# A graph network's layer ends: the third last superchunk's logits moved into the sums of its predecessor, and two merges moved behind a scaling

## The chip, the core and the metric

The kernel runs on one core of a Trainium2 chip. The core has five engines that work through lists of their own: TensorE (PE in the profile) for matrix products, VectorE (DVE) for elementwise work and scans, ScalarE (ACT) for activations and copies, GpSimd (POOL), which here only issues gathers, and SyncE (SP), which issues the other transfers. They wait for each other by semaphores. The metric is the device time of the whole program in microseconds, as the median over runs. One more execution is recorded by the profiler; its rows are what the prediction works with.

## The reference

The input is a graph of 6250 nodes with 256 features, and 200000 edges sorted by their target node, each with 32 features. Two attention layers run over it, the first with 4 heads, the second with 1. Cut to what matters:

```python
h = relu(layernorm(x))
for l in (0, 1):                        # heads 4 and 1
    te = relu(edge_attr @ We + be) * exp(h @ Wo + bo)[src][:, None]
    s2, d2, ea2 = add_self_loops(src, dst, te, n)     # loop: mean of te over a node's edges
    hx = (h @ Wg).reshape(n, H, F)
    al = leaky_relu((hx*a_s).sum(-1)[src] + (hx*a_d).sum(-1)[dst] + ((ea2@Wge).reshape(-1,H,F)*a_e).sum(-1), 0.2)
    al = exp(al - segment_max(al, dst)[dst])
    al = al / segment_sum(al, dst)[dst]
    out = segment_sum(hx[src] * al[:, :, None], dst) + b
    h = relu(out + h) if l == 0 else out + h + h_start
return x + h
```

So each edge needs a row of its source node, an attention logit, a softmax over all edges with the same target, and a weighted sum into that target.

## The kernel before

The sorted edges are cut into chunks of 128, and 24 chunks make a superchunk. There are 66 superchunks per layer, numbered s = 0 to 65; the last two are shorter, 17 chunks (64) and 10 chunks (65). One superchunk's edges reach at most 112 consecutive nodes, so that its weighted sums fit in one window of 128 rows.

For a superchunk the program does the following, and each step is a method of the class.

- `gather` issues one indirect transfer per chunk on POOL: 128 rows of the node table T of this layer, into the buffer G (line 1084). There are three G buffers, taken in turn.
- `nodes` loads the table rows and the inputs of the window's own nodes (`tw`, `xw`) by SP, into one of four places, taken in turn.
- `spread`, `parts`, `rphase1`, `rphase2`, `blocks` and `adst` build the edge part of the logits in the PSUM tile `zad`: comparisons and casts on DVE (lines 1210, 1211, 1325 to 1328), products on TensorE (1186, 1195, 1333, 1347), a relu on ACT (1187).
- `edge_rows` turns `zad` into rows per edge (1361) and sums parts (1365).
- `logits` forms the logits and scans them forwards and backwards within a partition (1377 to 1394). `ends` transposes the scans' ends on TensorE into the tile `lf` (1401). `links` scans these across partitions on DVE (1411, 1413) and has TensorE transpose the result back (1418). `maxima` takes the maximum per segment, ACT the exponential of the difference (1428 to 1452).
- `onehots` makes the matrix S that maps an edge to its row of the window (1312). `scale` multiplies G by the softmax weights (1483, in pieces if asked). `carried` adds what the predecessor had for a node that both share into the first row of G (1465 to 1473); it needs the predecessor's evicted sums.
- `sums` adds S times G over all chunks in PSUM (1495, two matmul records per chunk), `evict` copies the result to SBUF on ACT (1501).
- `finish` is the merge with the self loop: some twenty short operations on DVE and a few on ACT (lines 1512 to 1609). In layer 0 `rows1`, `rows2` and `rows3` then make the node's row for layer 1 (two transpositions, two products, an addition at line 575, an exponential) and store it by SP into T, into T1, which is a second copy of the table, and into two tables of window rows. In layer 1 `rows3` stores the output.

The order on every engine is the order in which these methods are called; nothing is rearranged by a scheduler. The method `edges` runs through the superchunks of layer 0 and then of layer 1. In step k it takes superchunk k from its logits to its sums, and beside that prepares the edge part of k+1 and merges k-1. The rows of k-1 are finished in step k+1 (the variable `late`).

The last three superchunks of a layer are taken together by `ending(a, b, c, pv, late, after)`: a is 63, b is 64, c is 65, pv is 62, late is 61, and after is the first superchunk of layer 1, or nothing at the end. Before the change the step of 62 ends with the merge of 61 and then the merge of 62, and `ending` begins with the logits of 63. At the first layer's end, 24 gathers for layer 1 are issued early, from T1, into the G buffer of 63 (`after["own"] = ... a["G"]`); they wait for the sums of 63 and for the stores of 61 and 62 into T1. The rows of the last three superchunks are not in T1 then. They are put in afterwards by products with a selection matrix, from rows of T that the last stores have written. The second superchunk of layer 1 is gathered from T and waits for the last of these stores.

`warm` issues a product whose result nobody reads. `index_on` makes the index tables of later superchunks in layer 0, some 14 short DVE operations at a time.

Of the kernel before, what the change touches and what calls it, by code (L numbers as in the profile page):

```python
# [81 lines left out]
class Kernel:  # L82
# [704 lines left out]
    def edges(self, ctx):  # L787
        nc = self.nc
        steps = self.steps
        if self.NS % 2:  # L790
            self.load_lb(1)
        pv = late = None
        self.ahead, self.rest = 1, None
        for k, st in enumerate(steps):
            nx = steps[k + 1] if k + 1 < len(steps) else None
            if st["s"] + 2 >= self.NS:
                continue
            for q in steps[k + 1:k + 3]:
                if q["L"] is st["L"] and "tw" not in q:
                    self.nodes(q)  # L800
            self.load_lb(k + 2)
            left = 99
            if self.ahead < len(self.groups):
                left = self.groups[self.ahead][0] - 2 - (self.ahead + 2 >= len(self.groups)) - k
            self.fresh = self.rest is None and left <= 3
            if self.fresh:
                gi = self.index_load(self.ahead, self.xp)
                self.rest = self.index_group(self.ahead, self.xp, gi)
            if st["L"].l and (st["s"] == 2 or st["s"] + 3 == self.NS) and not hasattr(self, "flag_i"):
                self.flag()  # L810
                if self.early:
                    self.window()
            if st["s"] + 3 == self.NS:
                self.ending(st, *steps[k + 1:k + 3], pv, late, steps[k + 3] if k + 3 < len(steps) else None)
                pv = late = None
                continue
            if k == 2:
                nx["own"] = steps[0]["G"]
            if k:
                if "G" not in nx:  # L820
                    self.gather(nx, st.get("behind"))
                drain(self.logits(st))
                self.ends(st)
                self.index_on(k, left, False)
            self.spread(nx)
            self.parts(nx)
            y = self.rphase1(nx)
            next(y)
            if k:
                self.links(st)  # L830
            if late:
                self.rows2(late)
            self.load_fl(k + 1)
            self.blocks(nx)
            if k:
                drain(self.maxima(st))
            drain(y)
            self.load_ea(k + 2)
            self.rphase2(nx)
            self.adst(nx)  # L840
            if "S" not in st:
                self.onehots(st)
            if k:
                drain(self.scale(st))
                self.carried(st)
                self.sums(st)
            if late:
                self.rows3(late)
                late = None
            self.onehots(nx)  # L850
            rows = self.edge_rows(nx)
            for gap in self.finish(pv) if pv else ():
                if gap:
                    next(rows, None)
            drain(rows)
            self.evict(st)
            if pv:
                self.rows1(pv)
                late = pv
            self.index_on(k, left, True)  # L860
            if k == 4 and self.early:
                self.lacking()
            if k >= 6:
                next(self.late, None)
                next(self.late, None)
            if st["s"] + 4 == self.NS:
                drain(self.finish(st))
            pv = st

    def index_on(self, k, left, late):  # L870
# [15 lines left out]
    def ending(self, a, b, c, pv, late, after):  # L886
# [10 lines left out]
        for q in () if after or self.early else (b, c):  # L897
            q["idx"] = idx = self.np_.tile([P, 1], I32, name="oidx")
            nc.vector.tensor_add(idx, self.base_f[:, q["s"]:q["s"] + 1], self.iota_m)
            nc.vector.memset(idx[0:1, :], 1 << 20)  # L900
        drain(self.logits(a))
        self.ends(a)
        self.spread(b)
        self.parts(b)
        y = self.rphase1(b)
        next(y)
        self.links(a)
        self.rows2(late)
        self.load_fl(k + 1)
        self.blocks(b)  # L910
        drain(self.maxima(a))
        self.rows3(late)
        drain(y)
        self.load_ea(k + 2)
        if after:
            self.warm(1, self.ps_1, "u", [P, 512])
        self.rphase2(b)
        self.adst(b)
        self.rows1(pv)
        if after:  # L920
            self.warm(1, self.ps_1, "u", [P, 512])
        n = a["C"]
        p, r = 5 * n // 12, n - 7
        drain(self.scale(a, cuts=(1, p, n)))
        drain(self.scale(a, cuts=(0, 1)))
        self.carried(a)
        self.rows2(pv)
        self.sums(a, (1, p))
        self.rows3(pv)
        drain(self.edge_rows(b))  # L930
        y = self.rphase1(c)
        next(y)
        self.sums(a, (p, p + 4))
        drain(y)
        self.load_ea(k + 3)
        self.sums(a, (p + 4, r))
        self.onehots(b)
        drain(self.logits(b))
        self.ends(b)
# [2 lines left out]
        self.rphase2(c)  # L942
        self.links(b)
        self.blocks(c)
        self.sums(a, (r, n), (0, 1))
        self.adst(c)
        if early:
# [920 lines left out]
```

## Time and profile before

| | us |
|---|---|
| median of the three runs | 4654.29 |
| lowest and highest of them | 4650.57, 4657.3 |
| the profiled execution | 4691.18 |
| span of its trace, first to last instruction | 4689.3 |

| engine | busy us | share of the span | instructions |
|---|---|---|---|
| PE | 2936.1 | 63% | 10096 |
| DVE | 2834.2 | 60% | 6211 |
| ACT | 534.1 | 11% | 1189 |
| POOL | 3000.1 | 64% | 3216 |

Every row in the prediction is from this one profiled execution. Rows of a timeline begin with the start in microseconds from the span's beginning and the duration; then come engine, line, operation, result and operands, shape and count; in brackets stands the time in which the engine was idle before it, and what ended that. "remote" and "another core or an unknown queue" mean that the profile doesn't show what ended it. Rows of the table by stretch begin with the stretch; then come its length, the busy time of PE, PEld, DVE, ACT and POOL with the number of instructions in brackets, the granted clock of TensorE as a share, the share of the transfer engines, and GB/s. In the page's groups the two figures behind the bar are the busy time in all and the mean of one in nanoseconds.

### The profile page before, as it was taken

What the parts mean: (1) busy time and instruction counts of PE and PEld (TensorE: products, weight loads), DVE (VectorE), ACT (ScalarE), POOL (GpSimd) and SP (SyncE); (2) the same over time, 40 slices, a digit from 0 to 9 for tenths busy, and PEclk for the clock granted to TensorE, in tenths of its full rate; (3) what the DMA queues carried; (4) which work ended last, traced back from release to release, by engine and by line L of the source; (5) the groups of instructions that cost most, each with busy time, mean ns of one, the idle gap of its engine ahead of it and who ended that gap; (6) DMA issues with size and microseconds to landing.
All of it is one profiled execution on the core that took longest, in us unless ns stands there. A gap on an engine that the chain in (4) does not pass through costs nothing.

```text
span 4689.3 us, 35036 instructions
## 1 busy us (share of the span) xinstructions
PE 2936.1 (63%) x10096; PEld 1851.6 (39%) x10096; DVE 2834.2 (60%) x6211; ACT 534.1 (11%) x1189; POOL 3000.1 (64%) x3216
## 2 busy tenths in 40 slices
PE   7766665666666666666666656656566565565656
PEld 5434343343343343343443333434334343343334
DVE  6666676676666666666665545545455554554546
ACT  4211111111111111111110000000000000000000
POOL 5466666666666666666646666666666666666664
PEclk8877777777777777777787767767767776767767
DMA  7344444444444444444444444444444444444442
GB/s 221 87 131 134 124 137 136 125 133 136 133 130 133 135 129 132 138 129 132 133 117 115 123 119 118 127 113 122 123 122 119 118 126 116 119 124 113 123 124 74
DMA packets 248234, 591.76 MB, mean 126 GB/s; under 512 B 65850, under 2 KB 105126, under 8 KB 247784
## 3 DMA queue, kind: packets, MB, share of 16 engines
q0 software_dynamic: 150048, 422.51, 34.2%
q1 hardware_dynamic: 97009, 164.82, 11.0%
q10 hardware_dynamic: 976, 2.12, 0.2%
q8 instruction: 81, 1.33, 0.1%
q14 instruction: 120, 0.98, 0.1%
HBM read 544.23 MB, written 45.36 MB: 126 GB/s over the span
## 4 chain that ended last, share of the span: by engine, by line
DVE 31%; PE 24%; issue 19%; another core or an unknown queue 14%; POOL 10%; ACT 1%; DMA 1%; SPq 0%; DVEq 0%; ACTq 0%; POOLq 0%
PE u L1495 16%; DVE G L1483 12%; POOL G L1084 10%; DVE S L1312 4%; PE y L1186 3%; DVE lb L1210 1%; DVE m L1433 1%; DVE rt L1361 1%; PE ps L570 1%; PE fin L570 1%; PE zad L1195 1%; DMA G<-T,src 1%; DVE al L1379 1%; DVE a3r L1326 1%
## 5 line engine op out<-in xcount | busy, mean ns | idle before, releaser
L1084 POOL DMA_INDIRECT G<-T,src x3066 | 2924.0, 954 | 1582.1 <-issue 886.6
L1495 PE MATMUL u<-G,S 128*128 128x270 f32 (+1 forms) x6212 | 1721.0, 435 | 763.5 <-issue 556.0
L1495 PEld LDWEIGHTS u<-G,S 128*128 128x128 f32 x6212 | 1319.2, 215 | 1100.2 <-issue 597.3
L1483 DVE TENSOR_TENSOR G<-G,kps 128x6144 f32<-128x6144 f32 (+6 forms) x149 | 854.1, 5739 | 0.0
L1186 PE MATMUL y<-ea,webd 64*128 64x256 f32 (+2 forms) x1056 | 454.5, 811 | 366.0 <-issue 353.2
L1411 DVE TENSOR_TENSOR_SCAN cl<-fl,cl,lf 4x129 f32<-4x129 f32 (+1 forms) x130 | 61.1, 470 | 855.4 <-remote 756.0
L1312 DVE TENSOR_TENSOR S<-kps,loc 128x3072 f32<-128x3072 f32 (+1 forms) x135 | 438.1, 3245 | 4.6
L1195 PE MATMUL zad<-R,wea 128*64 128x384 f32 (+1 forms) x1056 | 293.1, 694 | 155.4 <-ACT R L1187 98.2
L1186 PEld LDWEIGHTS y<-ea,webd 64*128 64x128 f32 x1056 | 161.6, 287 | 510.4 <-issue 493.3
L1501 ACT ACTIVATE U<-u 128x270 f32<-128x270 f32 (+1 forms) x130 | 51.0, 393 | 1959.1 <-remote 1409.1
L1187 ACT ACTIVATE R<-y,webd 128x1024 f32<-128x1024 f32 (+3 forms) x264 | 235.4, 892 | 329.9 <-PE y L1186 173.4
L1195 PEld LDWEIGHTS zad<-R,wea 128*64 128x64 f32 x1056 | 84.5, 180 | 410.4 <-issue 205.2
L1379 DVE TENSOR_TENSOR al<-G 128x96 f32<-128x96 f32 (+1 forms) x132 | 34.2, 259 | 236.6 <-remote 176.3
L570 PE MATMUL fin<-wg,h1T 128*128 128x260 f32 x264 | 126.3, 628 | 1.5 <-ACT h1T L1589 1.5
L1361 DVE STREAM_TRANSPOSE rt<-zad 128x768 f32<-128x768 f32 (+1 forms) x130 | 125.7, 967 | 2.4 <-PE zad L1347 2.4
L1333 PE MATMUL zad<-a,Q 128*128 128x12 bf16 (+1 forms) x132 | 24.4, 185 | 143.2 <-issue 103.5
L1401 PE MATMUL lf<-ident,fb 128*36 128x128 f32 (+1 forms) x132 | 46.0, 349 | 107.4 <-issue 62.7
L1210 DVE TENSOR_TENSOR lb<-lb,kps 128x1536 bf16<-128x1536 bf16 (+1 forms) x68 | 112.9, 1661 | 0.0
L1587 PE MATMUL fin<-ident,fb 128*128 128x128 f32 x132 | 45.0, 395 | 98.8 <-issue 97.0
L1587 PEld LDWEIGHTS fin<-ident,fb 128*128 128x128 f32 x132 | 24.7, 195 | 164.7 <-issue 160.1
L1526 ACT ACTIVATE mw<-mw,mg 128x2 f32<-128x2 f32 x66 | 19.7, 298 | 601.5 <-DVE mw L1522 529.7
L1347 PE MATMUL zad<-lb,aq 128*128 128x384 bf16 (+2 forms) x264 | 85.0, 414 | 0.0
(267 smaller groups left out, 2275.6 us busy)
## 6 DMA issues: line engine op xcount, KB each, us to landing
ea<-in_ea_dram SPq DMA_DIRECT2D x64, 768.0 KB
G<-T,src POOLq DMA_INDIRECT x3066
lb<-locrow SPq DMA_DIRECT2D x64, 384.0 KB
nd<-t1rows SPq DMA_DIRECT2D x66, 225.8 KB
tw<-nd SPq DMA_DIRECT2D x66, 225.8 KB
tw<-T SPq DMA_DIRECT2D x66, 117.2 KB
T<-t1rows SPq DMA_DIRECT2D x66, 113.8 KB
tw<-in_x_dram SPq DMA_DIRECT2D x66, 112.0 KB
```

The source lines that it names most:

```text
L570: self.product = self.nc.tensor.matmul(ps[:, :L.MW], hT[:, k, :], self.wg[L.l][:, k, :], start=(k == 0), stop=(k == 1))
L1084: g = nc.gpsimd.indirect_dma_start(out=G[:, c, 0:L.TW], out_offset=None, in_=st.get("from", self.T[L.l])[0:self.N, :], in_offset=bass.Indi ...
L1186: nc.tensor.matmul(y[:, i, :n], self.webd[l][r, :], ea[r, w], start=True, stop=True)
L1187: nc.scalar.activation(R[:, :, w], y[:, :, :n], AF.Relu, bias=self.be[l])
L1195: nc.tensor.matmul(st["zad"][i * PH:(i + 1) * PH, o], self.wea[l][0], R[:, i, w], start=True, stop=False)
L1210: V.tensor_tensor(lb[:, :, :n], lb[:, :, :n], self.k_part.unsqueeze(2).to_broadcast([P, i, n]), op=OP.is_equal)
L1312: nc.vector.tensor_tensor(st["S"][:, c0:c1, :], self.k_iota.unsqueeze(1).to_broadcast(w), self.loc[:, o + c0:o + c1].unsqueeze(2).to_broad ...
L1347: self.nc.tensor.matmul(st["zad"][:, o], st["aq"].rearrange("p k j -> p (k j)"), st["lb"][:, w], start=False, stop=True)
L1361: V.transpose(rv[:, :32 * c].rearrange("p (b n) -> p b n", b=2), z.rearrange("p (b n) -> p b n", b=2)[:, :, :16 * c])
L1379: V.tensor_add(zv, gr, G[:, :c, L.p:L.p + H])
L1483: nc.vector.tensor_tensor(v, v, pw[:, c0:c1, :].unsqueeze(3) .to_broadcast([P, c1 - c0, H, L.F]), op=OP.mult)
L1495: p = nc.tensor.matmul(st["u"][:, :L.W], S[:, i, :], G[:, i, 0:L.W], start=(j == 0), stop=(j == c - 1))
```

## The change

In the step of superchunk 62, the sums are issued in three parts, 16, 4 and 4 chunks. Between the parts go the edge rows, logits, ends and links of 63, and behind them its maxima. The merges of 61 and of 62 are no longer in this step. In `ending`, what stood at the head for superchunk 63 falls away, its scaling starts at once, and the two merges and the making of rows for 61 and 62 follow behind it, among the parts of 63's sums. The load of 65's node rows moves from the head of step 63 to behind the merge of 61, whose place in the ring it takes. The load of 64's and 65's flags moves into the step of 62. Two warm-up products of the first layer's end are dropped. It applies at the ends of both layers.

```diff
             for q in steps[k + 1:k + 3]:
-                if q["L"] is st["L"] and "tw" not in q:
+                if q["L"] is st["L"] and "tw" not in q and q["s"] + 1 < self.NS:
                     self.nodes(q)
...
-                self.sums(st)
+                self.sums(st, (0, 2 * C // 3 if st["s"] + 4 == self.NS else st["C"]))
...
             self.onehots(nx)
+            if st["s"] + 4 == self.NS:
+                drain(self.edge_rows(nx))
+                drain(self.logits(nx))
+                self.ends(nx)
+                self.sums(st, (2 * C // 3, 5 * C // 6))
+                self.links(nx)
+                self.sums(st, (5 * C // 6, C))
+                self.load_fl(k + 2)
+                drain(self.maxima(nx))
+                self.evict(st)
+                self.rest_left = left
+                late, pv = pv, st
+                continue
...
-            if st["s"] + 4 == self.NS:
-                drain(self.finish(st))
             pv = st
...
-        drain(self.logits(a))
-        self.ends(a)
+        n = a["C"]
+        p, r = 5 * n // 12, n - 7
         self.spread(b)
         self.parts(b)
         y = self.rphase1(b)
         next(y)
-        self.links(a)
-        self.rows2(late)
-        self.load_fl(k + 1)
         self.blocks(b)
-        drain(self.maxima(a))
-        self.rows3(late)
+        scaling = self.scale(a, cuts=(1, p, n))
+        next(scaling)
         drain(y)
         self.load_ea(k + 2)
-        if after:
-            self.warm(1, self.ps_1, "u", [P, 512])
+        self.sums(a, (1, p))
+        drain(scaling)
+        drain(self.scale(a, cuts=(0, 1)))
         self.rphase2(b)
         self.adst(b)
-        self.rows1(pv)
-        if after:
-            self.warm(1, self.ps_1, "u", [P, 512])
-        n = a["C"]
-        p, r = 5 * n // 12, n - 7
-        drain(self.scale(a, cuts=(1, p, n)))
-        drain(self.scale(a, cuts=(0, 1)))
+        rows = self.edge_rows(b)
+        for gap in self.finish(late):
+            if gap:
+                next(rows, None)
+        drain(rows)
         self.carried(a)
-        self.rows2(pv)
-        self.sums(a, (1, p))
-        self.rows3(pv)
-        drain(self.edge_rows(b))
+        self.nodes(c)
+        self.rows1(late)
+        self.sums(a, (p, p + 4))
+        self.rows2(late)
+        drain(self.finish(pv))
+        self.index_on(k, self.rest_left, True)
+        self.rows3(late)
         y = self.rphase1(c)
         next(y)
-        self.sums(a, (p, p + 4))
+        self.sums(a, (p + 4, r))
+        self.rows1(pv)
         drain(y)
         self.load_ea(k + 3)
-        self.sums(a, (p + 4, r))
+        self.rows2(pv)
         self.onehots(b)
         drain(self.logits(b))
         self.ends(b)
...
         self.links(b)
         self.blocks(c)
+        self.rows3(pv)
         self.sums(a, (r, n), (0, 1))
         self.adst(c)
```

## The prediction

> **What bounds the kernel now.** I read the page first, then the POOL and DVE timelines around the two layer ends, then the chain of waits and the busy time by stretch.
>
> ```profile
> span 4689.3 us, 35036 instructions
> L1084 POOL DMA_INDIRECT G<-T,src x3066 | 2924.0, 954 | 1582.1 <-issue 886.6
> L1312 DVE TENSOR_TENSOR S<-kps,loc 128x3072 f32<-128x3072 f32 (+1 forms) x135 | 438.1, 3245 | 4.6
> L1361 DVE STREAM_TRANSPOSE rt<-zad 128x768 f32<-128x768 f32 (+1 forms) x130 | 125.7, 967 | 2.4 <-PE zad L1347 2.4
> L1401 PE MATMUL lf<-ident,fb 128*36 128x128 f32 (+1 forms) x132 | 46.0, 349 | 107.4 <-issue 62.7
> ```
>
> A superchunk is 24 gathers of 0.95 us with 0.30 us between them (POOL rows below), 30 us, plus a wait for the sums that free the buffer: POOL paces the middle of both layers. The change leaves the 62 middle steps of each layer as they are. It can act only at the two layer ends (superchunk 63 is the third last, 64 the second last, 65 the last), and a shift at the first end moves all of layer 1 by the same amount.
>
> First end: the row before and after the gathers for layer 1, and the chain.
>
> ```profile
> 2382.72 0.94 POOL L1084 DMA_INDIRECT G<-T1e,src  x1 [20.35 <-PE zad L1347]
> ...
> 2411.66 1.10 POOL L1084 DMA_INDIRECT G<-T1e,src  x1 [0.30 <-issue]
> 2430.46 0.94 POOL L1084 DMA_INDIRECT G<-T,src  x1 [17.70 <-DMA T<-t1rows]
> ```
>
> ```profile
> 2400.19 10.10 another core or an unknown queue
> 2410.31 0.70 ACT R L1187
> ```
>
> POOL is idle 20.35 us until TensorE has finished the sums of 63; then come 24 gathers from T1, and then a wait for 65's rows in T. So what counts here is when the last sixteen matmuls of 63's sums end. What precedes them is DVE's list, from the one-hots of 63 to the links of 64, and in the second end the same list:
>
> ```profile
> 2336.64:2378.33 41.69, 32.38 (x135) 22.13 (x133) 35.16 (x104) 6.84 (x19) 15.79 (x17) 0.84 0.42 114
> 4617.93:4656.26 38.33, 26.43 (x119) 18.95 (x119) 26.61 (x65) 3.66 (x8) 18.31 (x20) 0.82 0.31 83
> ```
>
> The third busy figure is DVE's: 35.16 of 41.69 us, and 26.61 of 38.33. The new order permutes this list; it takes no work out of it. It can win only the idle part, and only where it does not put idle time elsewhere.
>
> **First end, part by part.** DVE's rows:
>
> ```profile
> 2346.23 0.45 DVE L1365 TENSOR_REDUCE ade<-rt 128x96 f32<-128x288 f32 x1 [0.99 <-DVE fa L1578]
> 2347.64 0.42 DVE L1582 SCALAR_TENSOR_TENSOR t1rows<-fa,t1rows 128x256 f32<-128x256 f32 x1 [0.96 <-DVE ade L1365]
> ...
> 2350.20 0.15 DVE L1512 TENSOR_SCALAR cnt<-U 128x1 f32<-128x1 f32 x1 [0.89 <-ACT U L1501]
> ...
> 2354.95 0.26 DVE L1377 TENSOR_TENSOR G<-rt,G 128x96 f32<-128x96 f32 x1
> ...
> 2356.77 0.69 DVE L1210 TENSOR_TENSOR lb<-lb,kps 128x544 bf16<-128x544 bf16 x1
> ...
> 2357.58 0.17 DVE L1325 CAST a<-tw 128x8 bf16<-128x8 f32 x1
> ...
> 2358.29 0.47 DVE L1411 TENSOR_TENSOR_SCAN cl<-fl,cl,lf 4x129 f32<-4x129 f32 x1
> ...
> 2377.39 0.47 DVE L1411 TENSOR_TENSOR_SCAN cl<-fl,cl,lf 4x129 f32<-4x129 f32 x1 [1.40 <-PE lf L1401]
> ```
>
> and TensorE's and ACT's:
>
> ```profile
> 2336.25 11.07 PE L1495 MATMUL u<-G,S 128*128 128x270 f32 x40 [3.00 <-DVE crow L1471]
> 2347.65 2.09 PE L1495 MATMUL u<-G,S 128*128 128x270 f32 x8 [0.33 <-issue]
> ...
> 2378.53 3.91 PE L1495 MATMUL u<-G,S 128*128 128x270 f32 x16
> ```
>
> ```profile
> 2349.77 0.40 ACT L1501 ACTIVATE U<-u 128x270 f32<-128x270 f32 x1 [1.71 <-PE u L1495]
> ```
>
> Waits that go: 0.99, 0.96, 0.89 and 1.40, together 4.24 us. Waits that come: with the one-hots (3.25), edge_rows of 63 (0.97 + 0.45) and its logits (2354.95 to 2356.77, 1.82) in a row, DVE is at 2343.1. The ends stand behind sixteen chunks of 62's sums, 32 matmuls at 11.07/40: 2345.1, plus 0.35 for the transposition, 2345.45. DVE waits 2.3 us. Its links take 0.94 (2377.39 to the window's end 2378.33), to 2346.4; the transposition back stands behind eight more matmuls, 2348.0: another 1.6 us. In the ending, blocks(b) comes straight behind parts(b) and waits for a product on TensorE with nothing between; no row has this pair alone, it is between 0 and the 0.7 that the casts take, I take 0.4. The casts for 65 (2357.58 to 2358.29, 0.7 us) become a second set, because 65's rows are no longer loaded when 64's casts run. The table row of 62 leaves the list (0.3). Sum: -4.24 + 2.3 + 1.6 + 0.4 + 0.7 - 0.3 = +0.5 us. The scaling starts some 9 us earlier, and both merges, the index steps and the table row of 61 are then done behind it: same work, same end.
>
> TensorE's two warm-up products go, the first part of 63's sums runs about 13 us earlier; what is left for the end is the same sixteen matmuls, 3.91 us behind the links of 64. ACT's pieces move with their merges and cost nothing while DVE leads. The two transpositions inside 62's sums delay the end of these by 0.7 us and so the ten gathers of 65; POOL's 20.35 us of idle time covers that.
>
> SP: 65's node rows (two loads) move from the start of step 63 behind the first merge, some 12 us ahead of the casts that read them; a landing is 3.4 us by the next rows, so they are covered, and would cost at most those 3.4. The flags' load moves forward behind 63's links; behind it wait only loads for layer 1. The four stores of 61 and of 62 come 9 us later. One of them is new on the path: 62's rows in T1, which the gathers at 2382.72 read, are now written behind the links of 64.
>
> ```profile
> 2369.80 0.41 DVE L575 TENSOR_TENSOR t1rows<-fin,bias 128x260 f32<-128x260 f32 x1
> ...
> 2427.06 0.43 DVE L575 TENSOR_TENSOR t1rows<-fin,bias 128x260 f32<-128x260 f32 x1 [0.46 <-PE fin L570]
> ```
>
> ```profile
> 2371.03 1.15 SPq L1630 DMA_DIRECT2D T1e<-t1rows  x1
> ```
>
> From a table row's start (2427.06) to the gather that its store releases (2430.46) it is 3.4 us; T1's store is the second one, 0.4 to 1.2 more. With 0.2 for blocks ahead, T1 is ready 4.0 to 4.8 us after the links; the sums are done 0.35 + 3.91 + 0.28 = 4.5 after. That is -0.5 to +0.3; I add 0.2. First end: **+0.7 us**, and everything behind it shifts along.
>
> **Second end.**
>
> ```profile
> 4621.21 0.21 DVE L1517 SCALAR_TENSOR_TENSOR mg<-U,cnt,tw 128x1 f32<-128x1 f32 x1
> ...
> 4633.01 0.22 DVE L1517 SCALAR_TENSOR_TENSOR mg<-U,cnt,tw 128x1 f32<-128x1 f32 x1 [7.99 <-ACT U L1501]
> ...
> 4636.29 0.20 DVE L1377 TENSOR_TENSOR G<-rt,G 128x24 f32<-128x24 f32 x1 [0.24 <-issue]
> ...
> 4641.57 6.67 DVE L1483 TENSOR_TENSOR G<-G,kps 128x2304 f32<-128x2304 f32 x3
> ...
> 4655.31 0.47 DVE L1411 TENSOR_TENSOR_SCAN cl<-fl,cl,lf 1x129 f32<-1x129 f32 x1 [1.29 <-PE lf L1401]
> ```
>
> ```profile
> 4617.88 10.83 PE L1495 MATMUL u<-G,S 128*128 128x261 f32 x48 [1.77 <-DVE G L1473]
> ```
>
> ```profile
> 4632.59 0.39 ACT L1501 ACTIVATE U<-u 128x261 f32<-128x261 f32 x1 [10.20 <-remote]
> ```
>
> Here there is something to win: 7.99 + 1.29 = 9.28 us of waits. But the 7.99 is odd: by the records 62's sums end at 4628.71, and ACT takes them only at 4632.59, 3.9 us later. In the middle of layer 1 the same is seen on the very wait that the change moves in here, the links' wait for the ends:
>
> ```profile
> 4596.94 0.27 PE L1401 MATMUL lf<-ident,fb 128*33 128x128 f32 x1
> ...
> 4608.05 0.39 ACT L1501 ACTIVATE U<-u 128x261 f32<-128x261 f32 x1 [20.19 <-remote]
> 4608.08 0.47 DVE L1411 TENSOR_TENSOR_SCAN cl<-fl,cl,lf 1x129 f32<-1x129 f32 x1 [16.45 <-remote]
> ```
>
> TensorE's record of the transposition ends at 4597.2, DVE gets it at 4608.08, together with ACT: a signal of TensorE is late while gathers run. After the change, logits of 63 end about 4623.4 (4617.93 + 3.25 + an estimated 2.2, the layer-0 pieces at a quarter of the width). The ends are recorded at 4617.88 + 10.83 x 32/48 + 0.35 = 4625.45.
> - Prompt signals: waits of 2.0 for the ends, 1.2 for the transposition back (eight matmuls of 0.23 and 0.35 later), 0.4 for blocks, 0.5 for edge_rows of 64 behind the first sums, and 0.7 of casts: -9.28 + 4.8 = -4.5 us.
> - All held until 4632.59: 9.2 + 0.4 + 0.5 + 0.5 + 0.7 - 9.28 = +2.0 us.
> - Each 3.9 late as the row shows, at the latest at 4632.59: 5.9 + 2.3 + 0.2 + 0.5 + 0.7 - 9.28 = **+0.3 us**. I take this one, since it is this stretch's own row.
>
> **Sum.** +0.7 + 0.3 = +1.0. The profiled execution (4691.18 us, 1.9 outside its span) would come to 4692.2; the median shown is 36.9 lower and the change is the same there: 4654.29 + 1.0 = **4655.3 us**.
>
> **Rivals.**
> - *Prompt signals in layer 1* (4.5 instead of 0.3): 0.7 - 4.5, 4650.5 us. For it: at 2349.77 ACT took 62's sums in layer 0 without delay. Against it: 4632.59 and 4608.08.
> - *A slow TensorE, on the other side.* Between the early sums and the last sixteen matmuls TensorE now mostly waits for DVE, and the warm-ups are gone. The profile shows what a gap does:
>
> ```profile
> 2350.00:2356.00 6.00, 0.00 (x0) 0.00 (x0) 5.11 (x23) 1.71 (x6) 4.77 (x5) 0.80 0.60 148
> 2356.00:2362.00 6.00, 3.97 (x13) 2.50 (x15) 5.39 (x21) 0.84 (x2) 4.47 (x6) 0.50 0.41 113
> ...
> 4583.30:4590.00 6.70, 6.65 (x17) 5.28 (x18) 6.12 (x13) 0.30 (x1) 5.09 (x6) 0.55 0.39 107
> ```
>
>   After six empty microseconds the granted clock is 0.50; at 0.55, 17 matmuls of the sums take 6.65 us, 0.39 each against 3.91/16 = 0.244. Sixteen cost 2.35 us more. In layer 0 that lies on the path to T1's gathers, in layer 1 ahead of the last superchunk's zad product, for which DVE waits: 4.7 us in all, 4660.0. It decides if the gap ahead of the sixteen is near the empty stretch of the row; I count about 3 us with only small products in it. [...]
> - *ACT is freed in the first end.* The 10.10 us in the chain are ACT waiting to read one more TensorE result while T1's gathers run; 65's sums follow. If the gathers start later against 64's work, that signal may be out before: up to 10.1 us, 4645.2.
>
> **How the numbers follow.** Forecast 0.40, prompt 0.30, slow TensorE 0.18, ACT freed 0.09, the rest unforeseen. This kernel's measurement can tell about 0.2% from no change, 4645.0 to 4663.6. Below lie half of ACT freed (0.045), a third of prompt, where other gains join it (0.10), and a twelfth of the forecast case (0.035): 0.18. Above lie a third of slow TensorE, where all signals are held as well (0.06), an eighth of the forecast case (0.05) and the unforeseen (0.03): 0.14. Within: 0.68. The range takes in ACT freed and the slow case with 3 us of spread: 4645 to 4663.
>
> **What would show it.** In the after trace: DVE's wait at line 1411's counterpart in step 62 (2.3 us in layer 0; 2.0, 5.9 or 9.2 in layer 1 tells prompt from held); the first gather from T1 within 1 us of where it was against the one-hots of 63, released by the sums or by T1's store; the granted clock in the last sixteen matmuls (1.00 or 0.5); ACT's 10.1 us still there. I am wrong if DVE's list is not the bound, or if the middle steps change their period.

## The result, and the profile after

| | median, us | lowest to highest | runs |
|---|---|---|---|
| before | 4654.29 | 4650.57 to 4661.45 | 11 |
| after | 4666.38 | 4658.14 to 4673.75 | 11 |

The change makes the kernel 0.26% slower: ratio 1.0026, 95% interval 1.0018 to 1.0034, or 12.1 us. The forecast was 4655.3 us, within 0.2% of no change, with a range of 4645 to 4663; the measured median lies 3.4 us above that range.

The two profiled executions cannot be compared as wholes. That of before took 4691.18 us, 37 us more than its median, and spread the excess over many middle steps, most of them in layer 0; that of after took 4673.75 us (span 4671.9). So I measure each layer end by itself, from the eviction of superchunk 61's sums to that of 63's. The lines of the changed kernel stand 12 further down behind `ending`. ACT's timeline at the two ends, before:

```profile
2323.25 0.40 ACT L1501 ACTIVATE U<-u 128x270 f32<-128x270 f32 x1 [10.84 <-PE u L1495]
...
2382.48 0.40 ACT L1501 ACTIVATE U<-u 128x270 f32<-128x270 f32 x1 [2.11 <-PE u L1495]
...
4660.28 0.39 ACT L1501 ACTIVATE U<-u 128x261 f32<-128x261 f32 x1 [2.67 <-PE u L1495]
```

and after:

```profile
2301.51 0.40 ACT L1513 ACTIVATE U<-u 128x270 f32<-128x270 f32 x1 [12.24 <-remote]
2329.48 0.40 ACT L1513 ACTIVATE U<-u 128x270 f32<-128x270 f32 x1
2366.26 0.40 ACT L1513 ACTIVATE U<-u 128x270 f32<-128x270 f32 x1 [4.32 <-PE u L1507]
...
4582.95 0.39 ACT L1513 ACTIVATE U<-u 128x261 f32<-128x261 f32 x1 [20.14 <-remote]
4612.39 0.39 ACT L1513 ACTIVATE U<-u 128x261 f32<-128x261 f32 x1 [2.60 <-PE zad L1345]
4643.07 0.39 ACT L1513 ACTIVATE U<-u 128x261 f32<-128x261 f32 x1 [4.76 <-PE u L1507]
```

The first end grows from 59.2 to 64.8 us (+5.5), the second from 52.2 (4608.05, shown in the prediction, to 4660.28) to 60.1 (+7.9). Together 13.4 us; the medians say 12.1. Most middle steps keep a period of 34 to 35 us, by the evictions (median 34.5 us before, 34.4 after).

Where each end grows is seen in DVE's list, in the same stretch as in the prediction: from the one-hots of 63 to the links of 64. The last two rows are the last sixteen matmuls of 63's sums at each end.

```profile
2314.89:2359.05 44.16, 34.45 (x129) 24.16 (x130) 35.02 (x106) 6.62 (x18) 15.54 (x17) 0.78 0.36 93
4592.84:4636.34 43.50, 29.43 (x117) 21.02 (x119) 27.02 (x68) 3.55 (x8) 18.09 (x20) 0.78 0.27 73
2359.90:2366.20 6.30, 6.30 (x19) 4.78 (x18) 4.26 (x10) 0.44 (x2) 0.00 (x0) 0.61 0.44 154
4637.10:4643.10 6.00, 6.00 (x19) 4.61 (x18) 3.33 (x8) 0.22 (x2) 0.00 (x0) 0.64 0.01 3
```

DVE has as much work as before (35.0 and 27.0 us busy; 35.16 and 26.61 before), but the stretches are 2.5 us (41.69) and 5.2 us (38.33) longer. What follows the links is 3.1 and 2.7 us longer: (64.75 - 13.38 - 44.16) - (59.23 - 13.39 - 41.69), and (60.12 - 9.89 - 43.50) - (52.23 - 9.88 - 38.33). That splits both losses into longer waits of DVE and slower last matmuls.

DVE's waits, from its timeline at the first end,

```profile
2326.16 0.47 DVE L1423 TENSOR_TENSOR_SCAN cl<-fl,cl,lf 4x129 f32<-4x129 f32 x1 [4.71 <-PE u L1507]
...
2343.94 0.81 DVE L1371 STREAM_TRANSPOSE rt<-zad 128x288 f32<-128x288 f32 x2 [1.74 <-remote]
```

at the second end,

```profile
4607.32 0.47 DVE L1423 TENSOR_TENSOR_SCAN cl<-fl,cl,lf 1x129 f32<-1x129 f32 x1 [8.57 <-remote]
...
4612.43 0.18 DVE L1352 TENSOR_TENSOR aq<-zad,quad 128x12 bf16<-128x12 f32 x1 [0.94 <-PE zad L1345]
...
4626.01 0.81 DVE L1371 STREAM_TRANSPOSE rt<-zad 128x288 f32<-128x288 f32 x2 [4.42 <-remote]
```

and TensorE's timeline there:

```profile
4592.79 8.99 PE L1507 MATMUL u<-G,S 128*128 128x261 f32 x32 [2.11 <-issue]
4601.62 0.27 PE L1413 MATMUL lf<-ident,fb 128*33 128x128 f32 x1
4601.73 1.93 PE L1507 MATMUL u<-G,S 128*128 128x261 f32 x8
4608.27 0.31 PE L1430 MATMUL lf<-ident,cl 33*128 33x33 f32 x1 [4.61 <-DVE cl L1425]
4608.51 3.85 PE L1507 MATMUL u<-G,S 128*128 128x261 f32 x8
...
4621.72 0.41 PE L1359 MATMUL zad<-lb,aq 128*128 128x288 bf16 x2
...
4634.33 0.42 PE L1413 MATMUL lf<-ident,fb 128*33 128x128 f32 x1 [4.40 <-DVE fb L1406]
...
4637.16 5.87 PE L1507 MATMUL u<-G,S 128*128 128x261 f32 x16
```

The ends of 63 are recorded as done at 4601.89 and the links see them at 4607.32. TensorE waits for the links in the middle of 62's sums and then does the last eight matmuls in 3.85 us, twice the 1.93 of the eight before; the granted clock is 0.50 there (4608.30 to 4612.30). 64's attention products are recorded as done at 4622.13, DVE sees them at 4626.01. The last sixteen take 5.87 us (3.79 before), at the first end 6.33 (3.91).

### The profile page after: what moved, and what is told of

Its sections match the earlier page's. It is cut to its first block, busy times and chain, and to the rows that moved or that the text cites. A ratio compares the mean times of both kernels' runs of the same rounds, so it can differ in the third digit from the quotient of the medians.

```text
span 4671.9 us, 35032 instructions
## 1 busy us (share of the span) xinstructions
PE 2964.7 (63%) x10092; PEld 1863.7 (40%) x10092; DVE 2834.8 (61%) x6219; ACT 530.2 (11%) x1189; POOL 2999.9 (64%) x3216
## 3 DMA queue, kind: packets, MB, share of 16 engines
q0 software_dynamic: 150048, 422.51, 34.5%
## 4 chain that ended last, share of the span: by engine, by line
DVE 38%; PE 26%; issue 17%; another core or an unknown queue 16%; POOL 1%; ACT 1%; DMA 1%; DVEq 0%; ACTq 0%; POOLq 0%
PE u L1507 17%; DVE G L1495 14%; DVE S L1324 5%; PE y L1198 3%; DVE lb L1222 2%; POOL G L1096 1%; DVE rt L1373 1%; DVE m L1445 1%; PE zad L1207 1%; PE ps L570 1%; PE fin L570 1%; DVE cl L1423 1%; DVE al L1395 1%; DVE al L1391 1%
## 5 line engine op out<-in xcount | busy, mean ns | idle before, releaser
L1391 DVE TENSOR_TENSOR al<-G 128x96 f32<-128x96 f32 (+1 forms) x132 | 34.4, 261 | 227.3 <-remote 173.4
L1430 PE MATMUL lf<-ident,cl 36*128 36x36 f32 (+1 forms) x132 | 39.5, 299 | 80.1 <-DVE cl L1425 79.8
L1430 PEld LDWEIGHTS lf<-ident,cl 36*128 36x128 f32 (+1 forms) x132 | 23.2, 176 | 166.0 <-DVE cl L1425 163.9
```

The lines of the kernel that those rows point to most:

```text
L1391: V.tensor_add(zv, gr, G[:, :c, L.p:L.p + H])
```

## The experiments

Two theories were open. **Half clock:** TensorE's clock falls in the gaps that the new order makes. **Late results:** DVE sees TensorE's results late, for one or more of three reasons: they stand behind other matmuls, TensorE is slower than its records say, or POOL's gathers hold the signal up. All ratios are against runs of the kernel before on the same chip; the two right columns are the length of each end by the evictions of 61 and 63.

| kernel | ratio (95% interval) | first end, us | second end, us |
|---|---|---|---|
| before | | 59.2 | 52.2 |
| after | 1.0026 (1.0018 to 1.0034) | 64.8 | 60.1 |
| e1 new order in layer 0 only | 1.0012 (1.0003 to 1.0020) | 63.3 | 53.1 |
| e2 new order in layer 1 only | 1.0011 (1.0003 to 1.0020) | 58.4 | 58.4 |
| e3 TensorE fed | 1.0019 (1.0010 to 1.0028) | 61.7 | 57.0 |
| e4 64's products first | 1.0013 (1.0004 to 1.0021) | 62.8 | 56.0 |
| e5 merge of 61 back | 1.0022 (1.0012 to 1.0032) | 68.4 | 56.4 |
| e6 e3, e4 and e5 | 1.0023 (1.0014 to 1.0033) | 62.4 | 58.3 |
| e7 links behind all sums | 1.0018 (1.0008 to 1.0027) | 62.9 | 56.3 |
| e8 layer 1: no POOL gathers | one run | 65.2 | 50.5 |
| e9 logits and one-hot blocks only | 0.9997 (0.9988 to 1.0006) | 57.1 | 49.7 |
| e10 layer 0: no POOL gathers | one run | 59.8 | 58.0 |
| e11 e3, e4 and e7 | 1.0014 (1.0005 to 1.0023) | 61.7 | 54.8 |
| e12 64's gathers in two batches | 1.0035 (1.0021 to 1.0048) | 63.6 | 61.0 |

Where the code of an end is the same, its length differs between executions: the new first end takes 63.3 to 65.2 us (after, e1, e8, e12), the new second end 58.0 to 60.1 (after, e2, e10), the old ones 58.4 to 59.2 and 52.2 to 53.1. A difference of 2 us in one of these lengths decides nothing by itself. The links' waits repeat far better (8.57 to 8.68 us at the second end, 4.68 to 4.91 at the first, wherever nothing was put in front of them and the 17 gathers stay), and the verdicts on late results rest on those. The other two terms do not repeat so well: where the code is the same, the wait for 64's transposition at the second end is 2.34 to 4.42 us (after, e2, e10), and the last sixteen matmuls take 5.87 to 6.15 us there and 5.49 to 6.33 at the first end (after, e1, e12).

**e1 and e2: one end at a time.**

```diff
-            if st["s"] + 4 == self.NS:
+            if st["s"] + 4 == self.NS and st["L"].l == 0:      # e2: == 1
```

and the same condition chooses the old or the new order in `ending`.

> The new order at layer 0's end alone; layer 1's end keeps the order of the kernel before. Read from the two traces by the evictions of 61 to 63 at that end (59.3 us before, 64.8 us after), theory: +5.6 us against the kernel before, 4659.9 us, and the last sixteen matmuls of 63's sums at layer 0's end take about 6.3 us, at layer 1's end about 3.8. Rival (the terms of the prediction hold here and the rest of the loss is somewhere else): +0.7 us, 4655.0 us.

> The new order at layer 1's end alone. Theory, from the same evictions (52.2 us before, 60.1 us after): +7.8 us, 4662.1 us; the links of 63 wait some 8.6 us, the transposition of 64's rows some 4.4 us, and the last sixteen matmuls take 5.9 us. Rival (the terms of the prediction): +0.3 us, 4654.6 us. If the two ends do not add up to the 12 us of the whole change, something outside them moves too.

Measured: 4657.59 us for e1 and 4658.38 for e2, against 4651.69: +5.9 and +6.7, by the ratios +5.6 and +5.1. Both ends lose, each in its own kernel, and together they make up about the 12 us. In e2 the links wait 8.68 us again; the wait for 64's transposition is 2.36, not 4.42, and e10, with the same code there, has 2.34; so some 2 us of that one belong to the single execution shown above.

**e3: feed TensorE.**

```diff
         self.rows2(pv)
+        self.warm(2 if after else 4, self.ps_y, "y", [P, 2, 512])
         self.onehots(b)
         drain(self.logits(b))
         self.ends(b)
+        self.warm(1, self.ps_y, "y", [P, 2, 512])
```

> The changed kernel, with products that nothing reads put on TensorE ahead of the last sixteen matmuls of 63's sums: two (layer 0) or four (layer 1) of 128x512 ahead of the transposition of 64's ends and one behind it. Theory (TensorE idles for some microseconds there and runs the sixteen at half clock, 6.33 and 5.87 us): the granted clock is 1.00 in the sixteen, they take 3.9 and 3.8 us, and the time falls by 2.4 + 2.1 = 4.5 us, to 4661.9 us. Rival (the clock is low for another reason, or the sixteen are not on the path): 4666.4 us.

Measured: 4660.16 us, 8.5 above the kernel before where the changed one is 12 above. The busy time by stretch, in the two groups of sixteen:

```profile
2357.40:2361.30 3.90, 3.90 (x19) 3.15 (x18) 3.67 (x10) 0.44 (x2) 0.00 (x0) 1.00 0.78 278
4626.60:4630.40 3.80, 3.80 (x19) 3.14 (x18) 3.35 (x8) 0.19 (x1) 0.00 (x0) 1.00 0.00 0
```

The clock is 1.00, where it was 0.61 and 0.64 in the changed kernel, and the sixteen take 3.91 and 3.79 us, as before the change. So the half clock is the gaps' doing, and cost 2.42 + 2.08 = 4.5 us in the sixteen of the execution shown above. What e3 and the changed kernel lose against the kernel before differs by 3 to 4 us, but the intervals overlap; the gain in time is likely, not shown.

**e4: order on TensorE's queue.**

```diff
+        self.rphase2(b)
+        self.adst(b)
         self.sums(a, (1, p))
         drain(scaling)
         drain(self.scale(a, cuts=(0, 1)))
-        self.rphase2(b)
-        self.adst(b)
```

> The changed kernel, with the products of 64's attention rows (rphase2 and adst) put ahead of the first eighteen matmuls of 63's sums instead of behind them. Theory A (DVE waits 4.42 us at layer 1's end and 1.74 us at layer 0's for the transposition of 64's rows because these products stand behind the sums): both waits go, 4666.4 - 6.2 = 4660.2 us. Theory B (a result of TensorE is seen late while gathers run, until 65's gathers end at about 4625): the wait at layer 1's end stays at 3 us or more although TensorE records the products some 4 us earlier, only the 1.74 us go, 4664.7 us.

Measured: 4657.9 against 4651.69 us. TensorE's and DVE's timelines at the second end:

```profile
4613.76 0.40 PE L1359 MATMUL zad<-lb,aq 128*128 128x288 bf16 x2
```

```profile
4618.34 0.81 DVE L1371 STREAM_TRANSPOSE rt<-zad 128x288 f32<-128x288 f32 x2
```

The transposition no longer waits, at either end, so theory A holds for this wait. It does not show that results are prompt: they had 4 us to arrive. But theory B's strict form is out: 65's ten gathers run until 4621.75 in e4, and the result is used at 4618.34. At the first end the removed 1.7 us shorten nothing that can be told from the spread.

**e5: give DVE the merge to do while it waits.**

```diff
-                drain(self.edge_rows(nx))
+                rows = self.edge_rows(nx)
+                for gap in self.finish(pv):
+                    if gap:
+                        next(rows, None)
+                drain(rows)
                 drain(self.logits(nx))
```

> The changed kernel, with the merge of 61 back in its old place, ahead of the logits and links of 63, so that DVE has work while the links wait for TensorE; it leaves the list behind the scaling. Theory (the links' wait, 4.7 us at layer 0's end and 8.6 at layer 1's, ends when TensorE's result is seen, whatever DVE does meanwhile): at layer 0's end the wait shrinks below 1 us and the end comes 4 us earlier; at layer 1's end it shrinks by the merge's 2.0 us, and half or more of that goes into the wait for 64's transposition, which hangs on TensorE. Sum -4 to -6, 4661.5 us. Rival (DVE's list is not the bound at these ends): the waits move and the time stays, 4666.4 us.

The merge leaves its place behind the scaling. Measured: 4663.97 against 4654.06 us, hardly better than the changed kernel. At the second end the wait shrinks as expected, from 8.6 to 6.35 us. The first end gets longer, 68.4 us: the links' wait falls to 0.49, but they start later, TensorE's transposition itself waits 2.94 us for DVE, 62's eviction comes 32.3 us behind 61's (28.0 after the change), and the wait for 64's transposition, 1.74 us in the changed kernel, is longer:

```profile
2345.98 0.81 DVE L1371 STREAM_TRANSPOSE rt<-zad 128x288 f32<-128x288 f32 x2 [5.43 <-remote]
```

My theory missed here: work put in front of a late result delays what follows it.

**e6: the three together.** It has the edits of e3, e4 and e5.

> The three edits together: TensorE fed ahead of the last sixteen matmuls, 64's attention products ahead of the first eighteen matmuls of 63's sums, and the merge of 61 back in its old place. If each edit takes away a cost of its own (traces: about 2.0 + 0.3 + 4 at layer 0's end, 1.5 + 2.4 + 1 at layer 1's), the time is 4666.4 - 11.2 = 4655 us, which is that of the kernel before (ratio 1.000 to 1.001). If they overlap, it stays above 4659.

Measured: 4663.49 against 4654.06 us; the three costs do not add up. The second end shows why:

```profile
4620.68 0.47 ACT L1201 ACTIVATE R<-y,webd 128x256 f32<-128x256 f32 x1 [5.10 <-remote]
```

```profile
4622.90 6.18 PE L899 MATMUL y<-ident 128*128 128x512 f32 x8 [0.68 <-ACT R L1201]
4628.91 0.27 PE L1415 MATMUL lf<-ident,fb 128*33 128x128 f32 x1
```

The filler products use a bank that ACT must have read first. ACT got that bank's product (recorded until 4617.26) 3.4 us late, so the filler ran late, and the links of 64 waited 7.03 us behind it.

**e7: no link in the middle of the sums.**

```diff
-                self.sums(st, (2 * C // 3, 5 * C // 6))
+                self.sums(st, (2 * C // 3, C))
                 self.links(nx)
-                self.sums(st, (5 * C // 6, C))
```

> The changed kernel, with the links of 63 behind all of 62's sums on TensorE's queue (sums in two parts instead of three). If TensorE's result is seen late because of what else the chip does then (a fixed moment), the links at layer 1's end wait the same 8.6 us, 62's eviction comes about 4 us earlier (4608 instead of 4612 on the changed kernel's clock), and the time is 4665 to 4666. If the signal comes some microseconds behind the end of whatever TensorE has in hand, the wait is 1.9 us longer at each end: 4670 us.

Measured: 4661.9 against 4654.06 us. 62's eviction comes 26.8 us behind 61's instead of 29.4, and DVE's links at the second end wait as long as ever:

```profile
4605.09 0.47 DVE L1422 TENSOR_TENSOR_SCAN cl<-fl,cl,lf 1x129 f32<-1x129 f32 x1 [8.67 <-remote]
```

That is 24.47 us behind 61's eviction (4580.62). In the changed kernel it is 4607.32 - 4582.95 = 24.37, in e2 to e6 24.4 to 24.5, though TensorE and DVE have different work around it. The moment is fixed by something else. The time forecast for that case, 4665 to 4666 us, can't be told from this: the loss is 7.8 us against 12.1, and the intervals overlap.

**e8 and e10: no gathers on POOL**, each in one layer only. The edit is shown without its condition on the layer; e10 loads from `self.T[0]`.

```diff
-        self.gather(b)
-        self.gather(c)
+        for q in (b, c):                                   # e8 in layer 1, e10 in layer 0
+            q["G"] = self.gp[q["k"] % 3].tile([P, C, 270], F32, name="G")
+            self.nc.sync.dma_start(q["G"][:, :q["C"], 0:q["L"].TW],
+                                   self.T[1][0:P * q["C"], :].rearrange("(c p) w -> p c w", p=P))
```

> The changed kernel, with POOL's 27 row gathers for 64 and 65 in layer 1 replaced by two plain loads of as many rows from SyncE's queue; they bring other rows, so the nodes of 64 and 65 are not computed. The loop ahead of it is the same. Theory (results and signals are seen late while POOL issues gathers): the links of 63 at layer 1's end wait about 2 us instead of 8.6, the recorded end of 64's attention products and the start of their transposition are within 0.5 us, and the last end is 6 us or more shorter. Rival (TensorE itself is slower than its records there, whoever moves the rows): the links still wait 6 us or more.

> The changed kernel, with POOL's 27 row gathers for 64 and 65 in layer 0 replaced by two plain loads of as many rows from SyncE's queue; they bring other rows, so the nodes of 64 and 65 get other values. Theory (POOL's gathers make results be seen late at layer 0's end too, but there the links also wait for TensorE, whose first matmuls run at half clock): the links of 63 follow the recorded end of the transposition within 0.6 us and wait 1 to 3 us instead of 4.7, and the wait for 64's transposition falls from 1.7 us to under 1. Rival (at this end only the half clock counts): both waits stay.

TensorE and DVE in e8, at the second end:

```profile
4601.56 0.27 PE L1418 MATMUL lf<-ident,fb 128*33 128x128 f32 x1
...
4616.55 0.41 PE L1364 MATMUL zad<-lb,aq 128*128 128x288 bf16 x2
```

```profile
4601.87 0.47 DVE L1428 TENSOR_TENSOR_SCAN cl<-fl,cl,lf 1x129 f32<-1x129 f32 x1 [3.42 <-PE lf L1418]
...
4617.00 0.81 DVE L1376 STREAM_TRANSPOSE rt<-zad 128x288 f32<-128x288 f32 x2 [0.95 <-PE zad L1364]
```

and DVE in e10, at the first end, where TensorE's transposition is recorded until 2321.68:

```profile
2321.72 0.47 DVE L1428 TENSOR_TENSOR_SCAN cl<-fl,cl,lf 4x129 f32<-4x129 f32 x1 [2.40 <-PE lf L1418]
```

Without POOL's gathers DVE starts 0.04 us behind the recorded end at both links, and the waits of 8.6 and 4.7 us fall to 3.42 and 2.40 (2 us were expected for the first). The transposition of 64's rows follows 0.04 us behind its product in e8 and does not wait in e10. The second end takes 50.5 us, the first 59.8. So in the changed kernel it is the gathers that make the results late. With prompt results the new order at the second end would be some 2 us shorter than the old one with its gathers (52.2 to 53.1), although its last sixteen still take 4.95 us; the first end would be about 1 us longer than the old. Both are single executions (4662.57 and 4660.43 us as a whole, too few to compare), within the spread given above. The old order without gathers was not run. TensorE could also simply have been slower than its records; the 0.04 us here speak against it where no gathers run. Where they run, the recorded starts do not show a slow TensorE either: in the changed kernel the eight matmuls behind the transposition start at 4601.73 and take 1.93 us, long before the links start at 4607.32. That the gathers hold up the end of a product and not its signal is not ruled out.

**e9: the part that fills a wait and makes none**, put into the kernel before.

```diff
             drain(rows)
+            if st["s"] + 4 == self.NS:
+                drain(self.logits(nx))
+                self.ends(nx)
+                self.spread(steps[k + 2])
             self.evict(st)
```

with the three calls taken out of `ending`.

> The kernel before, with a third of the change: only the logits of 63, the transposition of its ends and the one-hot blocks of 64 go ahead of 62's eviction and merge; the links of 63 and both merges stay where they were, and 62's sums stay whole. Theory (a gain is to be had only where DVE's moved work fills a wait and brings no earlier wait for TensorE): at layer 1's end the wait for 62's eviction falls from 7.8 us by about 2.4, and the wait for 63's ends (1.3) goes; at layer 0's end about 2 us of waits go: 4 to 6 us below the kernel before, ratio 0.9987 to 0.9991. Rival (DVE's list does not set these ends): ratio 1.000.

Measured: 4649.41 against 4651.2 us, ratio 0.9997: no difference that can be told. In the profile both ends are the shortest of all, 57.1 and 49.7 us, and DVE's wait for 62's eviction is 5.92 us, 2.1 less than the 7.99 before. The 1.3 us that I expected to go from the wait for the ends are in the prediction the wait for 64's (4655.31), not for 63's; it falls to 0.69 us here. The row of the 5.92 us:

```profile
4595.75 0.22 DVE L1518 SCALAR_TENSOR_TENSOR mg<-U,cnt,tw 128x1 f32<-128x1 f32 x1 [5.92 <-ACT U L1502]
```

Against the old ends (58.4 to 59.2 and 52.2 to 53.1) that would be some 4 to 6 us, the gain expected; the interval of the ratio reaches from -5.6 to +2.8 us, so the runs neither show it nor exclude it.

**e11: the edits of e3, e4 and e7 together**, with three more filler products at the second end, in a bank that nothing reads.

> The changed kernel with the three edits that each shortened an end in the traces: the links of 63 behind all of 62's sums, 64's attention products ahead of the first eighteen matmuls of 63's sums, and TensorE fed ahead of the last sixteen (two products and one at both ends, three more at layer 1's end, in a bank on which nothing waits). If the account of the loss is complete, they give back 2 + 2.5 us at layer 0's end and 2 + 2.4 + 2 at layer 1's: 11 us, which leaves 1 us above the kernel before (ratio 1.000). If something not yet named costs time, the ratio stays above 1.001.

Measured: 4658.26 against 4651.2 us, 1.0014. By these figures somewhat under half of the loss is given back (7.1 us remain of 12.1) and not the 11 us expected, so the account behind that figure was not complete; the interval overlaps with that of the changed kernel. The sixteen take 3.91 and 3.79 us and the wait for 64's transposition is gone; the links of 63 still wait 4.68 and 8.64 us, and none of the three edits touches that.

**e12: end the batch earlier.**

```diff
-        self.gather(b)
+        self.gather(b, None if after else lambda i: a["turn"] if i >= 9 else None)
```

where `a["turn"]` is the transposition of 63's ends on TensorE.

> The changed kernel, with the last eight of 64's 17 gathers in layer 1 made to wait for the transposition of 63's ends on TensorE; nothing else moves. In every run so far that has POOL's 17 gathers there, the links of 63 at layer 1's end start 24.4 to 24.5 us after the eviction of 61 (changed kernel: 4607.32 - 4582.95), some 3 us after the last of the 17 gathers, wherever their ends stand on TensorE's queue. Theory (a result is seen when the running batch of gathers is through): with a batch of nine, which ends 11.3 us after the eviction, the links start as soon as the ends are recorded, 19 to 20 us after the eviction, wait about 3.5 us instead of 8.6; the eighteen gathers that follow then make the next results late, so the wait for 64's transposition stays or grows, and the time is 4662 to 4667 us. Rival (the moment is set by TensorE or by something else in the step): the links still start 24.4 us after the eviction.

Measured: 4709.2 us against 4692.11 for the kernel before, run beside it, 1.0035. Both stand some 40 us above the other sets; why is not known. The loss of 17.1 us is more than the expected time allows (4662 to 4667 us, some 8 to 13 above the kernel before), though its interval overlaps with that of the changed kernel. DVE at the second end, and POOL:

```profile
4633.01 0.47 DVE L1423 TENSOR_TENSOR_SCAN cl<-fl,cl,lf 1x129 f32<-1x129 f32 x1 [3.45 <-PE lf L1413]
...
4658.86 0.48 DVE L1371 STREAM_TRANSPOSE rt<-zad 128x288 f32<-128x288 f32 x1 [11.66 <-remote]
```

```profile
4624.02 0.95 POOL L1096 DMA_INDIRECT G<-T,src  x1 [0.30 <-issue]
4633.24 0.94 POOL L1096 DMA_INDIRECT G<-T,src  x1 [8.28 <-PE lf L1413]
...
4654.56 0.94 POOL L1096 DMA_INDIRECT G<-T,src  x1 [0.30 <-issue]
```

The links start 19.2 us behind 61's eviction (4613.79) instead of 24.4, 0.04 us behind the recorded end of the transposition (4632.97). The theory of the links holds, and its second half too: the eighteen gathers that now run on without a break from 4633.24 make the next result late. 64's products are recorded as done at 4648.11, DVE sees them at 4658.86, 3.36 us after the last gather (4655.50). In the changed kernel it is 3.18 us, from the last of 64's gathers to the links:

```profile
4603.19 0.95 POOL L1096 DMA_INDIRECT G<-T,src  x1 [0.30 <-issue]
```

## Why the prediction was wrong, step by step

**What held.** The middle steps keep their period. DVE's work is only permuted. The gathers from T1 are still released by the sums and not by the store of 62's rows:

```profile
2366.49 0.94 POOL L1096 DMA_INDIRECT G<-T1e,src  x1 [24.48 <-PE zad L1359]
```

ACT's late result at the first end stays (8.72 us instead of 10.10), so the rival "ACT is freed" was wrong.

**"What is left for the end is the same sixteen matmuls, 3.91 us behind the links of 64"** is the step that failed at both ends. They are the same sixteen, but at a granted clock of 0.61 and 0.64, and take 6.33 and 5.87 us; with the small products ahead of them this is the +3.1 and +2.7 found above. The slow-TensorE rival had the mechanism and the price, 2.35 us per end against 2.42 and 2.08. I gave it 0.18 because I counted only 3 us of gap. The clock fell without six empty microseconds like those in the prediction's row (2350 to 2356), as the row just ahead of the sixteen at the second end shows:

```profile
4631.00:4637.10 6.10, 1.97 (x11) 1.18 (x11) 5.13 (x16) 0.00 (x0) 0.00 (x0) 0.51 0.06 19
```

TensorE is busy for a third of the stretch and the clock is 0.51. At the first end there was less idle time still. The stretch ahead of the sixteen there, and the longest wait of TensorE in it:

```profile
2355.40:2359.90 4.50, 1.93 (x12) 1.17 (x12) 3.52 (x17) 0.00 (x0) 0.00 (x0) 0.75 0.56 117
```

```profile
2357.00 0.30 PE L1413 MATMUL lf<-ident,fb 128*36 128x128 f32 x1 [1.64 <-DVE fb L1406]
```

The clock is 0.95 until 2357 and 0.50 from 2358 to 2364. At the second end 4.40 us are idle in one piece (4634.33 above), at the first end no piece is longer than 1.64 us, and the clock fell in both. How short a gap lets it fall was not measured, nor how little work keeps it up, beyond e3's products, which did (1.00). Of the last eight matmuls of 62's sums at the second end the prediction knew nothing: they follow the 4.61 us that TensorE waits for the links, and take 3.85 us at a clock of 0.50, 1.9 more.

**The waits at the second end.** The prediction took 5.9 us for the ends, 2.3 for the transposition back, 0.5 for 64's transposition and 0.2 for the blocks; measured were 8.57, 0.41, 4.42 and 0.94. That is +5.4 us, and the stretch grew by 5.2; some 2 us of it, in the 4.42, did not come again in e2 and e10. Two steps fail here. The late signal was sized by one row, 3.9 us behind TensorE's record, when what counts for the links is when the batch of gathers is through: e12, with nine gathers, and e8, with none, show it, both 0.04 us behind the record. The bound "all held until 4632.59" (9.2 us) was the right choice for the links. And one move was not priced: in the new `ending` 64's attention products stand behind the first eighteen matmuls of 63's sums. With that, their result comes while 65's gathers run; e4 takes the wait away by the order alone.

**The waits at the first end.** The sum was +0.5 us and the stretch grew by 2.5. The wait for the ends is 4.71 us instead of 2.3. The sixteen chunks of 62's sums take longer than the 8.9 us of the prediction (11.07 x 32/40): 10.60 us in the trace of after, where the clock is 0.50 in the first 4 us, 9.20 in e10, and the result is seen 0.9 us late in after and at once in e10. The 1.74 us for 64's transposition had no term, as at the second end. The transposition back costs 0.34 us and not 1.6; "4.24 us of waits removed" was right.

**The two signs.** Prompt results would have made the second end a gain: e8 is 1.8 to 2.7 us shorter than the old end, and 1.2 us more with its sixteen at full clock (4.95 against 3.79), where the rival of prompt signals had 4.5. The row against that rival (4608.08) was in the prediction, 11 us late; I priced by the row that was 3.9 us late. And the row for it (2349.77, in layer 0) lay behind its batch: 64's 17 gathers are issued there from 2323.49 to 2344.63, and at the pace found below they are through at 2347.8, an estimate.

## What to carry to other kernels

Before a wait on another engine is moved, look at what POOL does at that moment: in this kernel a result that fell late into a batch of 17, 18 or 24 gathers was seen 3.2, 3.4 and 4.4 us behind the last of them, so the price of the new wait can run to there, and the old place may have been hidden behind work. When early work is pulled away from in front of a last group of matmuls, price that group at the clock that the new gap leaves it (here 0.61 and 0.64, 6.33 and 5.87 us instead of 3.91 and 3.79). And list every call whose order on each queue changes, not only those that the change is about: the products that nobody meant to move cost a wait as well (1.74 and 4.42 us in the changed kernel, none in e4).

## What the runs showed of the hardware

I had not expected the late results to be tied so exactly to the gathers. In nine executions with 17 gathers on POOL and the links in their new place (after, e2 to e7, e10, e11) the links at the second end start 24.4 to 24.5 us behind 61's eviction, whatever else was changed; with nine gathers (e12), or none on POOL (e8, and e10 at the first end), 0.04 us behind TensorE's recorded end. In the three batches that I measured the time behind the last gather is not the constant, the time per gather is. From the first gather of a batch to the moment it is 24.1 us for 17 gathers (4583.19 to 4607.32), 25.6 for the 18 of e12 (4633.24 to 4658.86) and 34.3 for 24 in a middle step of the kernel before (4573.76 to 4608.05): 1.42 to 1.43 us each, where POOL's records stand 1.25 apart. So the tail grows with the batch, 3.2, 3.4 and 4.4 us. The first and the last gather of the 24:

```profile
4573.76 0.95 POOL L1084 DMA_INDIRECT G<-T,src  x1 [4.38 <-remote]
...
4602.75 0.95 POOL L1084 DMA_INDIRECT G<-T,src  x1 [0.30 <-issue]
```

It is no strict rule. In the changed kernel, 3.0 us into the batch of 17, ACT takes a product recorded until 4586.21 at 4586.26. And in 65's batch of ten at the second end, 64's products were seen 3.2 us late in e2, e3 and e10 and 1.7 us in e5, before the last gather had ended. In e10 they are recorded until 4610.90 and used at 4614.08; the tenth gather ends at 4615.1 there, an estimate from the changed kernel, where it ends 12.5 us behind 62's eviction (4602.54 in e10).

Why results are seen late while a batch runs stays open, but two rows narrow it down. In the last 1.5 us or so before the links of the changed kernel, neither POOL nor the transfer engines show any work (the last two columns are the transfers' share and rate):

```profile
4605.70:4607.20 1.50, 0.00 (x0) 0.00 (x0) 0.00 (x0) 0.00 (x0) 0.00 (x0) 1.00 0.00 0
```

And in e10, while the plain loads keep the transfer engines full,

```profile
2331.00:2338.40 7.40, 6.45 (x28) 4.30 (x27) 6.85 (x19) 1.05 (x3) 0.00 (x0) 0.88 1.13 345
```

64's products are recorded until 2337.45 and DVE uses them 0.99 us later, at 2338.44, without a wait. So the traffic alone does not explain it; what POOL does behind its records is not in the profile. Middle steps show the same thing: by the rows in the prediction, TensorE's transposition at 4596.94 is seen at 4608.08, together with ACT's operand, and POOL's own wait between two batches ends at such a moment too. Here it is at the start of 64's gathers in the changed kernel, 0.24 us behind 61's eviction (4582.95):

```profile
4583.19 0.94 POOL L1096 DMA_INDIRECT G<-T,src  x1 [4.55 <-remote]
```

Whether that time, in a step of some 34 us, can be had was not tried.
